# A graph-attention layer's lead-in: constant products, query weights in pieces, four tiles' queries first, and an earlier adjacency pass

## The chip, the cores and the metric

The kernel runs on one core of a Trainium2 chip. A core has five engines that run side by side, each through its own list of instructions in order: TensorE (PE, matrix products, with its weight loads PEld), VectorE (DVE), ScalarE (ACT), GpSimd (POOL) and SyncE (SP, which here only issues transfers). Transfers (DMA) are issued by SP, ScalarE and GpSimd. The engines wait for each other and for transfers by semaphores. The metric is the device time of one execution in microseconds (us); less is better.

## What is computed

One graph-attention layer over 16 batches of 1024 nodes with 512 features, with a residual and a layer normalisation without gain:

```python
# x (16, 1024, 512) f32, adj (1024, 1024) of 0 and 1, Wq Wk Wv Wo (512, 512), biases (512)
q = (x @ Wq + bq).reshape(b, n, 8, 64)
k = (x @ Wk + bk).reshape(b, n, 8, 64)
v = (x @ Wv + bv).reshape(b, n, 8, 64)
scores = einsum('bqhd,bkhd->bhqk', q, k) / sqrt(64)
scores = scores + (1.0 - adj)[None, None, :, :] * -1e9
attn = softmax(scores, axis=-1)
out = einsum('bhqk,bkhd->bqhd', attn, v).reshape(b, n, 512)
x = layernorm(x + out @ Wo + bo)          # mean and variance over the last axis, eps 1e-5
```

The adjacency is sparse and the same for all batches; a query has few keys, some have none.

## The kernel before

**Sorting the queries.** Because the adjacency is sparse, the kernel computes no full score matrix. It first sorts the 1024 queries by their number of keys. The generator `ranks` (L461) loads the eight adjacency tiles of 128 rows and makes one pass over them: `most` (L456) multiplies a tile with the column numbers and takes the eight largest on VectorE (`keys`, `asked`), and sums the row on ScalarE (`key_of`). From the sums it makes a sort key per query (L474), spreads the keys by TensorE (`pkeys`, L479) and copies them on ScalarE (L481), counts for each query on VectorE how many keys are smaller (L491, one instruction per tile of queries), and scatters the rows of `asked` to `order` in memory by these ranks (L485). Then TensorE turns the ranks (`pranks`, L503), and SP reads `order` back as `ranked` (L504). `asked_row` (L511) then says which query stands where, and gathers of everything else use it.

**Edges.** Queries with many keys get further lists: `edges(t)` (L637) for tiles 7 and 6 gathers the adjacency rows of the sorted tile (`codes`, L641), takes the largest again and again on VectorE, and turns edges into rows of keys and queries with small products on TensorE (`poff`, `pe`, `pof`), one-hot sums on VectorE (L711 to L723) and a copy on ScalarE (L730). `lookups` (L593) gathers the keys' places by GpSimd.

**Queries, keys and values of a batch.** The 1024 rows of x come in eight tiles of 128; `pair(b, j)` (L816) does two tiles. A tile is loaded (L750), turned by four transposes on TensorE and copied on ScalarE to `xT` (`transpose_x`, L752). A product of a tile with a 512 x 512 matrix is four matmuls (`product`, L793). `out_q` (L825) scales a tile of queries and adds the bias on VectorE, and SP writes it to memory. The first pair of the first batch computes keys and values plainly (`plain`, L923; `pk`, `pv`, with the outputs copied on ScalarE). All other pairs use a scheme with fewer products: sums and differences of the tiles and of the weights (`combine`, L780; `T1` to `T4`, L383 to L388) and seven units of two matmuls (`unit`, L948) in the accumulators x, p6, p7, z and p4. Their outputs depend on each other: `e` is copied from x on ScalarE (L969) before x is used again, `w` and `g` are sums on VectorE (L972, L975), and z is used a second time only after the V of the odd tile has been taken from it on VectorE (`out_v1`, L984). Transposes of the next pair stand inside the pair's list.

**Blocks.** The attention itself runs in blocks of 128 (query, key) pairs: GpSimd gathers keys and values, VectorE multiplies and reduces to scores (L1313, L1317), ScalarE takes exponentials and weighs values (L1328, L1341), VectorE or TensorE adds up, and TensorE does the output product (`po`).

**What sets the order.** The kernel writes the order of each engine's instructions itself. A loop over places `n` runs from -39 (`LEAD_IN`) to beyond the last block (L1538); block n belongs to place n, and places below 0 are the lead-in. At each place come, in this order: the functions that earlier ones have planned for this place (`later`, L448; then `later_last`), then units of TensorE's work from the list `fronts` until the place's credit is used up (3.3 us at the assumed costs up to place -14, then 2.0), and then one step of each preparing generator: `loads` (L357), `ranks`, and further on `edges`, `checks`, `lookups` and the bias set-up. A `yield` in a generator ends its step. The constants at the top say at which places these start: `ADJ_AT` has the places of the adjacency pass, `REST_FROM` those of the edges of tiles 7 and 6. A unit may have a condition; if it isn't met, the place ends there. Since each engine works in order, an instruction that has to wait holds up all that stand behind it on its engine.

**Loads.** At place -39 `loads` issues Wq in one transfer of 1 MB and the query bias, on ScalarE's queue; at -38 Wk and Wv in halves (`B11`, `B21`, `B12`, `B22`); five places on, `wo` and ten small transfers that fill rows with zeros (L371 to L380); then come T1, T2 and T3, T4 on VectorE, and the other biases. x's first three tiles are issued by SP at the start, and each further one when a transpose has freed a buffer.

**Buffers.** Accumulators of TensorE for products, transposes and small work (`fill_psum`, L262) are four and go round; a fifth user waits until the first one has been read.

Of the kernel before, what the change touches and what calls it, by code (L numbers as in the profile page):

```python
# [10 lines left out]
F32 = mybir.dt.float32  # L11
# [39 lines left out]
ROWS = 3  # L51
# [4 lines left out]
FRONT_BY = -14  # L56
SEGMENT = 64
TOP = 8
ADJ_AT = {-36: (0,), -35: (1, 2), -34: (3, 4), -33: (5,), -32: (6, 7)}
CHECKS_AT = -27  # L60
BIAS_AT = -8
MORE_RANKS_AT = 1
NORMS_AT = 18
LOOK_FROM = -17
REST_FROM = {7: -24, 6: -6}

PRODUCT = 0.86
SUM = 0.87
# [6 lines left out]
P = 128  # L75
# [103 lines left out]
def kernel(  # L179
# [36 lines left out]
    nc = tc.nc  # L216
    B, N, D = x.shape
    HD = D // HEADS
    NPAIR = D // P
# [22 lines left out]
    W = {}  # L242
# [9 lines left out]
    def load_w(t, w):  # L252
        nc.scalar.dma_start(t, w.rearrange("(c p) e -> p c e", p=P))

    with ExitStack() as main:
# [6 lines left out]
        def fill_psum(name):  # L262
            return psum.tile([P, HALF], F32, tag="fill", name=name, bufs=4)
# [92 lines left out]

        def loads():  # L357

            load_w(W["q"], wq)
            broadcast(bq_bc, bq)  # L360
            nc.vector.tensor_scalar(bq_bc, bq_bc, scale, None, op0=OP.mult)
            yield

            B12[0] = work.tile([P, 2, D], F32, tag="kv", name="b12", bufs=5)
            load_w(B11, wk[0:HD2, :])
            load_w(B21, wk[HD2:D, :])
            load_w(B12[0], wv[0:HD2, :])
            load_w(B22, wv[HD2:D, :])
            for _ in range(5):
                yield  # L370
            load_w(W["o"], wo)  # L371
            for rows in solo_rows + pair_rows:
                for r in range(N, rows.shape[0], N + 1):
                    nc.scalar.dma_start(rows[r:r + 1, 0:D], zeros[0:1, 0:D])
            for i in range(1, ROWS):
                nc.scalar.dma_start(q_rows[i][ds(ONE_KEY * P, P), :], zeros[:, 0:D])
                if i % B >= PAIRED_FROM and not merged(i):
                    nc.scalar.dma_start(q_rows[i][0:P, :], zeros[:, 0:D])
            left = P - 8 * (B - PAIRED_FROM)
            nc.scalar.dma_start(more_rows[P - left:, :], zeros[0:left, 0:D])  # L380
            nc.vector.tensor_scalar(before, place[:, 0:P], -1.0, query[:, 0:1], op0=OP.add, op1=OP.is_gt)
            yield
            nc.vector.tensor_tensor(T1, B12[0], B11, op=OP.subtract)  # L383
            nc.vector.tensor_tensor(T2, B22, T1, op=OP.subtract)
            combined.append(True)
            yield
            nc.vector.tensor_tensor(T3, B22, B12[0], op=OP.subtract)
            nc.vector.tensor_tensor(T4, B21, T2, op=OP.subtract)  # L388
            yield
            broadcast(bo_bc, bo)  # L390
            nc.scalar.dma_start(bias_rows[0:NPAIR, :], bq.rearrange("(c p) -> c p", p=P))
            nc.scalar.dma_start(bias_rows[NPAIR:, :], bk.rearrange("(c p) -> c p", p=P))
            nc.scalar.dma_start(bv_rows, bv.rearrange("(c p) -> c p", p=P))
# [54 lines left out]
        def later(k, fn):  # L448
            plan.setdefault(now[0] + k, []).append(fn)
# [11 lines left out]
        def ranks():  # L461
# [11 lines left out]

            nc.vector.scalar_tensor_tensor(key, asked[:, :, 1], float(N), query, op0=OP.mult, op1=OP.add)  # L474
            nc.vector.tensor_copy(keys.rearrange("p (t q) -> p t q", t=NT), key[:, :, None].to_broadcast([P, NT, P]))
            yield
            pk = [fill_psum(f"pkeys_{i}") for i in range(2)]
            for t in range(NT):
# [273 lines left out]
        def transpose_x(b, t):  # L752
            def pe():
                xs = X.pop((b, t))
                p = fill_psum(f"pxT_{b}_{t}")
                for c in range(NPAIR):
                    nc.tensor.transpose(p[:, ts(c, P)], xs[:, ts(c, P)], ident)  # L757

                def out():
                    XT[b, t] = work.tile([P, D], F32, tag="xT", name=f"xT_{b}_{t}", bufs=4)  # L760
                    nc.scalar.copy(XT[b, t], p)
                    n = b * NT + t + 3
                    if t == 0 and b >= PAIRED_FROM:
                        if not merged(b):
                            BOTH[b // 2] = work.tile([P, 2, NPAIR, P], F32, tag="place", name=f"both_{b}", bufs=1)
                        nc.scalar.copy(
                            BOTH[b // 2].rearrange("p w c (h n) -> p h c w n", h=2)[:, b % 2],
                            p.rearrange("p (c w n) -> p c w n", c=NPAIR, w=2),
                        )
                        sq = work.tile([P, D], F32, tag="ysq", name=f"sq_x_{b}", bufs=1)  # L770
                        nc.scalar.activation(sq[0:LONE, :], xs[0:LONE, :], AF.Square, accum_out=x_norm[0:LONE, b:b + 1])
                    if b * NT + t in STORED:
                        nc.sync.dma_start(residual[b * NT + t], xs)
                        later(2, lambda: load_x(n // NT, n % NT))
                    else:
                        load_x(n // NT, n % NT)
                    if t % 2 and (b, t) != (0, 1):
                        later(1, combine)

                def combine():  # L780
                    s = [work.tile([P, HD2], F32, tag=f"s{i}", name=f"s{i}_{b}_{t}", bufs=1 + i // 4) for i in (1, 2, 3, 4)]
                    x0, x1 = XT[b, t - 1], XT[b, t]
                    nc.vector.tensor_tensor(s[0], x1[:, 0:HD2], x1[:, HD2:D], op=OP.add)
                    nc.vector.tensor_tensor(s[2], x0[:, 0:HD2], x1[:, 0:HD2], op=OP.subtract)
                    nc.vector.tensor_tensor(s[1], s[0], x0[:, 0:HD2], op=OP.subtract)
                    nc.vector.tensor_tensor(s[3], x0[:, HD2:D], s[1], op=OP.subtract)
                    SX[b, t // 2] = s

                later(1, out)

            return [(TRANSPOSE, pe, lambda: (b, t) in X)]

        def product(name, lhs, w, out):  # L793

            def unit(c):
                if c == 0:
                    PS[name] = fill_psum(name)
                p = PS[name]
                nc.tensor.matmul(p, lhs(c), w[:, c, :], start=(c == 0), stop=(c == NPAIR - 1))  # L799
                if c == NPAIR - 1:  # L800
                    del PS[name]
                    later(1, lambda: out(p))

            return [(PRODUCT, lambda c=c: unit(c), None) for c in range(NPAIR)]
# [11 lines left out]
        def pair(b, j):  # L816
# [5 lines left out]
                KV[b, tt[i]] = work.tile([P, 2 * D], F32, tag="kv", name=f"kv_{b}_{tt[i]}", bufs=5)  # L822
                return KV[b, tt[i]]

            def out_q(i, p):  # L825

                assert gathered[0] >= start[max(0, b - ROWS + 1)]
                tag, bufs = ("q", 2) if b or j else ("y", Y_BUFS)
                q = work.tile([P, D], F32, tag=tag, name=f"q_{b}_{tt[i]}", bufs=bufs)
                nc.vector.scalar_tensor_tensor(q, p, scale, bq_bc, op0=OP.mult, op1=OP.add)  # L830
                later(1, lambda: nc.sync.dma_start(q_rows[b % ROWS][ds(tt[i] * P, P), :], q))

            def out_k(i, p):
                kv = new_kv(i)
# [72 lines left out]
            def lhs(i):  # L907
# [3 lines left out]
                product(f"pq_{b}_{tt[i]}", lhs(i), W["q"], lambda p, i=i: out_q(i, p)) if b == 0 or tt[i] != ONE_KEY else []  # L911
                for i in range(2)
            )
            if j == 0 and b >= PAIRED_FROM:
                q0 = []
                if merged(b):
                    q0 = product(f"pq_{b}_0", lambda c: BOTH[b // 2][:, 1, c, :], W["q"], lambda p: out_q(0, p))
                    q0 += lone_product()
# [3 lines left out]
            if (b, j) == (0, 0):  # L922
                def plain(i, name, top, bottom, out):  # L923
                    def unit(c):
                        if c == 0:
                            PS[name] = fill_psum(name)
                        w = top() if c < 2 else bottom
                        nc.tensor.matmul(PS[name], XT[b, tt[i]][:, ts(c, P)], w[:, c % 2, :], start=(c == 0), stop=(c == 3))
                        if c == 3:
                            p = PS.pop(name)  # L930
                            later(1, lambda: out(i, p))

                    return [(PRODUCT, lambda c=c: unit(c), None) for c in range(NPAIR)]

                units = q0 + q1 + xt
                for i in range(2):
                    units += plain(i, f"pk_{i}", lambda: B11, B21, out_k)
                for i in range(2):
                    units += plain(i, f"pv_{i}", lambda: B12[0], B22, out_v)
                return units  # L940
# [53 lines left out]
            units = []  # L994
# [520 lines left out]
        prep.setdefault(LOOK_FROM, []).append(lookups())  # L1515
        with tc.manual_schedule():

            fronts += transpose_x(0, 0) + transpose_x(0, 1)
            fronts_by = []
            for b in range(B):  # L1520
                for j in range(NT // 2):
# [136 lines left out]
```

## Time and profile before

| what | value |
|---|---|
| median of 3 runs | 1845.04 us (1844.67 to 1846.6) |
| profiled execution: its time, its span | 1842.18 us, 1840.4 us |
| TensorE busy | 1798.2 us, 98% of the span |
| VectorE busy | 1693.7 us, 92% |
| ScalarE busy | 1563.2 us, 85% |
| GpSimd busy | 1215.3 us, 66% |
| granted TensorE clock, mean | 0.996 |
| moved by DMA | 558.54 MB, mean 303 GB/s |

A row of the profile that speaks of instructions names the line in the kernel, the engine and the operation, then the tile written and the tiles read, their shapes, and the number of instructions; in brackets stands how long the engine stood idle before it, and what ended that. A row of the waits names who waited for whom, the total, the number of times and the longest. A row of the chain is a start, a length and what ran then: the chain is followed back from the last instruction, at each step to what released it. A matmul of 128x512 in f32 shows as two records. `pp` stands for p6, p7 and p4 alike, and `b`, `t`, `s` for the weights and sums of the scheme.

### The profile page before, as it was taken

Reading aid. Unit: us, or ns where it says so; the run is one execution under the profiler, and the core shown is the slowest. Engines: PE = TensorE matmul, PEld = TensorE weight load, DVE = VectorE, ACT = ScalarE, POOL = GpSimd, SP = SyncE. Lnnn points to the kernel's source line nnn. Section 1 sums busy time; section 2 is a strip of 40 time slices with the busy share of each in tenths; the row PEclk is TensorE's granted clock in tenths of the full one; section 3 lists DMA queues with packets and bytes.
Section 4 is the critical chain, followed back from the end, with each engine's and each line's share of the span. In section 5 each row is a group of like instructions: output and inputs, shape, how many; then the busy total and the mean of one; then the engine's idle time right before and its main releaser. Section 6 shows DMA issues by size and latency. Waiting matters only on the chain.

```text
span 1840.4 us, 25352 instructions
## 1 busy us (share of the span) xinstructions
PE 1798.2 (98%) x5140; PEld 876.2 (48%) x5140; DVE 1693.7 (92%) x3473; ACT 1563.2 (85%) x6183; POOL 1215.3 (66%) x1142
## 2 busy tenths in 40 slices
PE   7999999999999999999999999999999999999997
PEld 3444454554444454444444445444544444444443
DVE  6889889999989999999999999999999999997986
ACT  3637869989889898999889988989799999987886
POOL 1367766766565776767757666677666767665786
PEclk9999999999999999999999999999999999999998
DMA  7358787989889899999988998999989999889995
GB/s 287 106 190 253 256 325 237 346 301 327 308 280 314 295 336 319 344 316 308 347 316 310 346 335 276 343 321 322 339 315 325 314 355 326 306 324 325 338 319 191
DMA packets 198791, 558.54 MB, mean 303 GB/s; under 512 B 33450, under 2 KB 33470, under 8 KB 198626
## 3 DMA queue, kind: packets, MB, share of 16 engines
q0 software_dynamic: 112640, 370.50, 59.3%
q1 hardware_dynamic: 82910, 180.52, 26.2%
q10 hardware_dynamic: 3076, 5.82, 0.9%
q14 instruction: 122, 1.00, 0.2%
q8 instruction: 43, 0.70, 0.2%
HBM read 420.30 MB, written 157.45 MB: 314 GB/s over the span
## 4 chain that ended last, share of the span: by engine, by line
PE 69%; DVE 10%; ACT 9%; DMA 4%; issue 3%; POOL 1%; SPq 0%; POOLq 0%; DVEq 0%; ACTq 0%
PE po L799 17%; PE pq L799 15%; PE pp L956 12%; PE z L956 9%; PE x L956 9%; ACT pv L1341 5%; DVE qk L1313 2%; PE poT L1401 2%; PE pxT L757 2%; PE sum L1367 2%; DVE s L1317 2%; PE sum L1366 2%; DVE pv L1357 1%; ACT sq_k L809 1%; DMA kvg<-kv_pair,place_row 1%
## 5 line engine op out<-in xcount | busy, mean ns | idle before, releaser
L1341 ACT ACTIVATE pv<-kvg,pv 128x64 f32<-128x64 f32 x3600 | 907.5, 341 | 0.0
L1292 POOL DMA_INDIRECT kvg<-kv_pair,place_row x462 | 526.7, 1140 | 307.4 <-ACT pv L1341 99.6
L799 PE MATMUL pq<-wq,xT 128*128 128x512 f32 x792 | 367.8, 596 | 0.0
L1317 DVE TENSOR_REDUCE s<-qk 128x8 f32<-128x512 f32 x530 | 360.7, 681 | 6.8
L799 PE MATMUL po<-wo,oT 128*128 128x512 f32 x792 | 359.3, 594 | 0.7 <-ACT oT L1405 0.7
L1313 DVE TENSOR_TENSOR qk<-qt,kvg 128x512 f32<-128x512 f32 x434 | 297.2, 685 | 1.1 <-DMA kvg<-kv_rows,key_row 0.6
L956 PE MATMUL x<-b,xT 128*128 128x512 f32 x504 | 237.3, 593 | 0.5 <-ACT e L969 0.4
L956 PE MATMUL pp<-t,s 128*128 128x512 f32 x504 | 237.0, 593 | 0.0
L1357 DVE TENSOR_TENSOR pv<-pv,pv 128x520 f32<-128x520 f32 x329 | 228.3, 694 | 4.3 <-ACT pv L1341 4.2
L799 PEld LDWEIGHTS po<-wo,oT 128*128 128x128 f32 x792 | 149.1, 191 | 170.0 <-issue 160.2
L799 PEld LDWEIGHTS pq<-wq,xT 128*128 128x128 f32 x792 | 148.4, 192 | 161.9 <-issue 149.9
L1010 POOL DMA_INDIRECT x<-in_x_dram,asked_row x120 | 133.0, 1108 | 77.8 <-issue 21.3
L1148 POOL DMA_INDIRECT out_dram<-y,asked_row x129 | 146.9, 1139 | 39.1 <-issue 21.2
L1328 ACT ACTIVATE pv<-s,absent 128x8 f32<-128x8 f32 x434 | 127.0, 294 | 44.0 <-DVE s L1317 40.8
L809 ACT ACTIVATE sq_k<-kv 128x128 bf16<-128x128 f32 x512 | 150.8, 301 | 6.4 <-DVE kv L979 3.4
L956 PEld LDWEIGHTS pp<-t,s 128*128 128x128 f32 x504 | 94.7, 191 | 108.1 <-issue 99.4
L956 PEld LDWEIGHTS x<-b,xT 128*128 128x128 f32 x504 | 94.2, 191 | 107.4 <-issue 99.0
L956 PE MATMUL z<-b,s 128*128 128x512 f32 x252 | 119.2, 596 | 7.0 <-DVE kv L984 7.0
L1246 POOL DMA_INDIRECT qg<-q_rows,query_row x96 | 104.4, 1088 | 28.4 <-issue 26.9
L956 PE MATMUL z<-t,s 128*128 128x512 f32 x252 | 118.6, 593 | 0.0
L956 PE MATMUL pp<-t,xT 128*128 128x512 f32 x252 | 118.5, 593 | 0.0
L1134 ACT ACTIVATE y<-y,stats 128x512 f32<-128x512 f32 (+1 forms) x128 | 102.7, 806 | 17.0 <-DVE stats L1129 17.0
(279 smaller groups left out, 2713.0 us busy)
## 6 DMA issues: line engine op xcount, KB each, us to landing
kv_pair<-kv SPq DMA_DIRECT2D x98, 512.0 KB
q_rows<-q SPq DMA_DIRECT2D x106, 256.0 KB
qt<-q_rows SPq DMA_DIRECT2D x98, 256.0 KB
residual<-x SPq DMA_DIRECT2D x83, 256.0 KB
y<-residual SPq DMA_DIRECT2D x83, 256.0 KB
kv_rows<-kv SPq DMA_DIRECT2D x15, 512.0 KB
kvg<-kv_pair,place_row POOLq DMA_INDIRECT x462, 6.9
kv_pair<-kv SPq DMA_DIRECT2D x28, 256.0 KB
```

Source lines behind the costliest of these rows:

```text
L799: nc.tensor.matmul(p, lhs(c), w[:, c, :], start=(c == 0), stop=(c == NPAIR - 1))
L809: nc.scalar.activation(sq, s[:, ts(h, P)], AF.Square, scale=scale, accum_out=sums[:, h:h + 1])
L956: nc.tensor.matmul(R[bank], l[:, ts(c, P)], right[:, c, :], start=(first and c == 0), stop=(c == 1), skip_group_check=True,)
L1010: nc.gpsimd.indirect_dma_start(out=y, out_offset=None, in_=x_rows, in_offset=bass.IndirectOffsetOnAxis(ap=asked_row[:, t:t + 1], axis=0), ...
L1148: nc.gpsimd.indirect_dma_start(out=out_rows[b, t], out_offset=bass.IndirectOffsetOnAxis(ap=rows, axis=0), in_=y, in_offset=None, element_o ...
L1246: nc.gpsimd.indirect_dma_start(out=q, out_offset=None, in_=q_rows[b % ROWS], in_offset=bass.IndirectOffsetOnAxis(ap=rows, axis=0))
L1292: nc.gpsimd.indirect_dma_start(out=KG[n], out_offset=None, in_=rows, in_offset=bass.IndirectOffsetOnAxis(ap=(place_row if b else key_row)[ ...
L1313: nc.vector.tensor_tensor(QK[n], q, KG[n][:, 0:D], op=OP.mult)
L1317: nc.vector.tensor_reduce(S[n], QK.pop(n).rearrange("p (h d) -> p h d", d=HD), axis=AX.X, op=OP.add)
L1328: nc.scalar.activation(PV[n][:, D:], S.pop(n), AF.Exp, bias=bias)
L1341: nc.scalar.activation(pv[:, ts(h, HD)], v[:, ds(D + h * HD, HD)], AF.Copy, scale=pv[:, D + h:D + h + 1])
L1357: nc.vector.tensor_tensor(PV[b, t], PV[b, t], pv, op=OP.add)
```

## The change

Six edits, all of them before place 0:

- Two new units at the head of TensorE's list: `busy(3)`, three 128x512 products of a constant (`neg_one`, spread to 128x128 and 128x512) into an accumulator that nobody reads, then the transposes of tile 0, then `busy(1)`, one such product. The transposes of tile 1 move from there to behind the queries of tile 0.
- Wq is loaded in four transfers of 128 rows each, in place of one.
- The queries of tiles 2 and 3 (`pq_0_2`, `pq_0_3`) move from the second pair's list, where they stood between the units of the scheme, into the first pair's, ahead of its keys. The list is now: queries 0, transposes 1 and 2, queries 1, transposes 3, queries 2, queries 3, keys, values. `when(t, ...)` makes a group wait for the turned tile. `out_q` takes the tile's number from its new parameter.
- `ADJ_AT`: tile 0 of the adjacency pass at place -38 and the last two at -33; before, -36 and -32.
- Two more `yield` between the sort keys (L475) and `pkeys`. With the pass ending one place sooner, the sort keys come one place sooner (-32) and `pkeys` and all that follow in `ranks` one place later (-29 for -30, and so on). `REST_FROM` starts the edges of tile 7 one place later (-23), after `asked_row` is known.
- `loads` waits four places in place of five before `wo` and the zero rows; T1 to T4 and the biases come a place sooner with it.

```diff
+WARM = 3, 1
-ADJ_AT = {-36: (0,), -35: (1, 2), -34: (3, 4), -33: (5,), -32: (6, 7)}
+ADJ_AT = {-38: (0,), -37: (1,), -36: (2,), -35: (3,), -34: (4, 5), -33: (6, 7)}
...
-REST_FROM = {7: -24, 6: -6}
+REST_FROM = {7: -23, 6: -6}
...
-            load_w(W["q"], wq)
+            for c in range(NPAIR):
+                nc.scalar.dma_start(W["q"][:, c, :], wq[ds(c * P, P), :])
...
-            for _ in range(5):
+            for _ in range(4):
                 yield
             load_w(W["o"], wo)
...
             nc.vector.tensor_copy(keys.rearrange("p (t q) -> p t q", t=NT), key[:, :, None].to_broadcast([P, NT, P]))
+            yield
+            yield
             yield
             pk = [fill_psum(f"pkeys_{i}") for i in range(2)]
...
-            def out_q(i, p):
+            def out_q(i, p, j=j):
...
+            if (b, j) == (0, 1):
+                q0 = q1 = []
...
-                units = q0 + q1 + xt
+                def when(t, units):
+                    cost, fn, _ = units[0]
+                    return [(cost, fn, lambda: (0, t) in XT)] + units[1:]
+
+                q2, q3 = (
+                    product(f"pq_0_{t}", lambda c, t=t: XT[0, t][:, ts(c, P)], W["q"], lambda p, t=t: out_q(t % 2, p, 1))
+                    for t in (2, 3)
+                )
+                units = when(0, q0) + transpose_x(0, 1) + xt[:1] + when(1, q1) + xt[1:] + when(2, q2) + when(3, q3)
...
-            fronts += transpose_x(0, 0) + transpose_x(0, 1)
+            def busy(n):
+                def pe():
+                    p = fill_psum(f"busy_{n}")
+                    for _ in range(n):
+                        nc.tensor.matmul(p, neg_one.to_broadcast([P, P]), neg_one.to_broadcast([P, D]), start=True, stop=True)
+
+                return [(0.01, pe, None)]
+
+            fronts += busy(WARM[0]) + transpose_x(0, 0) + busy(WARM[1])
```

More of the change, by code (lines that the diff above doesn't have):

```diff
@@ L823, in new_kv @@
                 return KV[b, tt[i]]
-            def out_q(i, p):
+            def out_q(i, p, j=j):
                 assert gathered[0] >= start[max(0, b - ROWS + 1)]
                 tag, bufs = ("q", 2) if b or j else ("y", Y_BUFS)
-                q = work.tile([P, D], F32, tag=tag, name=f"q_{b}_{tt[i]}", bufs=bufs)
+                t = 2 * j + i
+                q = work.tile([P, D], F32, tag=tag, name=f"q_{b}_{t}", bufs=bufs)
                 nc.vector.scalar_tensor_tensor(q, p, scale, bq_bc, op0=OP.mult, op1=OP.add)
-                later(1, lambda: nc.sync.dma_start(q_rows[b % ROWS][ds(tt[i] * P, P), :], q))
+                later(1, lambda: nc.sync.dma_start(q_rows[b % ROWS][ds(t * P, P), :], q))
             def out_k(i, p):
```

## The prediction

> **What bounds the kernel now.** I read the page first, then who waits for whom on TensorE, then stretches of time, then the chain, then the timelines of the first 150 us. TensorE is busy for 1798.2 of 1840.4 us, so the end moves only by what the lead-in does to TensorE's idle and slow time. The list of TensorE's waits (us in total, times, longest us):
>
> ```profile
> PE pxT L757 <- DMA x<-in_x_dram: 7.1, 2, 4.2
> PE z L956 <- DVE kv L984: 7.0, 5, 3.0
> ...
> PE pk L928 <- DMA b<-in_L_gnn_Wk_dram: 2.0, 1, 2.0
> ...
> PE pranks L503 <- DVE rank_row L495: 1.3, 1, 1.3
> ```
>
> Two waits for x (7.1) and one for the key weights (2.0) are what the change aims at; the second line is what may come in their place. Stretches (TensorE, its weight loads, VectorE, ScalarE, GpSimd busy us; then granted clock, DMA share, GB/s):
>
> ```profile
> 10.00:20.00 10.00, 10.00 (x27) 4.78 (x26) 3.04 (x6) 2.58 (x5) 0.56 (x1) 1.00 1.04 415
> 20.00:30.00 10.00, 8.03 (x15) 3.17 (x14) 9.79 (x11) 4.82 (x10) 0.00 (x0) 0.83 0.82 322
> 30.00:40.00 10.00, 10.00 (x25) 4.47 (x24) 9.83 (x10) 3.73 (x17) 0.00 (x0) 1.00 0.57 188
> 40.00:62.00 22.00, 20.35 (x67) 9.94 (x66) 20.77 (x41) 12.82 (x31) 6.42 (x6) 1.00 0.25 86
> 62.00:120.00 58.00, 58.00 (x157) 26.64 (x157) 47.87 (x149) 28.96 (x88) 23.53 (x24) 1.00 0.42 146
> ```
>
> From 20 to 62 VectorE is as full as TensorE (40.4 of 42 us). From 10 to 20 the transfers are full. After 62 TensorE stands still for nothing until 130. Now the chain:
>
> ```profile
> 60.47 1.26 DVE keys L491 x2
> 61.73 0.08 DVE rank_row L495
> 61.81 0.07 issue
> 61.88 0.27 PE pranks L503
> ...
> 125.86 4.28 DMA codes<-in_adj_dram,asked_row
> 130.21 1.11 issue
> 131.31 0.70 DVE qk L1313
> ...
> 144.18 0.69 DVE kv L984
> 144.92 1.98 PE z L956 x4
> ```
>
> So two stretches belong to VectorE: the sorting of queries (keys, pkeys, ranks; 45 to 62) and the one from the transfer of codes to a V tile (126 to 145). A lead of TensorE at 36 us is worth what these two let through. ScalarE's timeline holds one more limit:
>
> ```profile
> 33.58 3.23 ACTq L376 DMA_DIRECT2D q_rows<-zeros  x2
> 36.85 0.44 ACTq L378 DMA_DIRECT2D q_rows<-zeros  x1
> 37.33 0.46 ACTq L380 DMA_DIRECT2D more_rows<-zeros  x1
> 37.84 1.06 ACT L459 ACTIVATE key_of<-adj 128x1024 f32<-128x1024 f32 x1 [6.27 <-DMA q_rows<-zeros]
> ```
>
> ScalarE issues wo and ten small transfers in a row; the second of the two q_rows issues starts at 36.45, when wo has just landed (36.43 in the trace's record of landings). Everything behind it, the key sums of the adjacency pass included, waits.
>
> **The Trainium skill.** The Trainium skill, "TensorE: Matmul & The Clock Gate", section What's actually happening: half clock after an idle window of about 3.4 us, full after a busy one, windows running freely. The trace agrees: a clock of 0.83 over 20 to 30 is one window of 3.4 us at half, and products run at half pace from 23.3 to 26.7 after the wait for Wk. The Trainium skill, "DMA: Bandwidth & Descriptors", section Issuing engines are not separate DMA queues: all transfers share the same 16 engines and interleave, so earlier requests only reorder bytes. It agrees: share 1.04 at 415 GB/s.
>
> **The change, part by part.**
>
> *Constant products.* Three products, each two passes (a product of 128x512 shows as two records). Cold, passes stand 0.86 us apart (four products = 6.9 us), warm 0.43. They start once neg_one is set (1.0 us) and take 3 x 1.72 = 5.2 cold, some 4.7 if the clock comes up meanwhile. x's first tile landed at 4.05, so its transposes go from 4.18 to 5.7: later by 1.5. But the first query product had waited for the second x tile (8.17) and now follows the first, at 5.7 + 0.5 (transpose) + 0.8 (fourth constant product, which covers the copy) = 7.0 instead of 9.1, and warm. The half pace from 9.1 to 13.1 cost 2.0.
>
> *Wq in four pieces.* The whole landed at 7.48; the pieces use the same queue in order, so the last is there at about 7.5, needed at 9.6: nothing gained or lost but three issues of 0.46 on ScalarE, hidden by its wait for the first transpose.
>
> *Order.* q0 7.0 to 10.5; T1; T2 (x landed at 10.97) to 11.5. The copy of T1 stands behind the first adjacency sum on ScalarE (adjacency tile 0 lands at 10.8, sum 1.15), so q1 starts at about 12.7. q1, T3, q2, q3 end at 23.4, two keys and two values (four products of 3.44) at 37.2. Wk and Wv are asked for 3.4 us sooner (after the first copy, not the second), landing at some 19 and 27, so the waits for Wk (2.0 idle, 1.7 half pace) go. Before, the same work, with q2 and q3 (6.9), was done at 36.5 + 6.9 = 43.4. **TensorE leads by about 6 us here.**
>
> *Adjacency pass.* On VectorE it starts at 10.9 (adjacency 0) instead of 18.7. Work up to the keys: 8 x 2.52 + four query outputs 2.4 + sums of x 1.45 + mask 0.3 + T1 to T4 4.9 + key 0.9 = 30.1, so 41.0 (before: 18.7 to 45.6, without query outputs).
>
> *wo one step sooner.* The run of eleven issues begins at 19 instead of 31, behind Wk and Wv. Bytes up to wo's end: adjacency 4.1 MB, x 1.8, Wq and bq 1.3, Wk and Wv 2.0, wo 1.0, queries 0.6 = 10.8; 1.8 are through at 8.2, the rest at about 400 GB/s: wo lands at 30 to 31. ScalarE is then free at about 32 (1.4 more as before), owes four sums (4.8), two key copies (1.0), two sets of squares (2.4) and two value copies (1.0) before e of the first fast pair: about 42.2. TensorE is there at 40.6 (37.2 + two units of 1.72). Wait 1.6; pkeys, now two places later, start at 42.2 + 1.7 = **43.9 instead of 45.69**.
>
> *Ranks.* From pkeys to the first rank 2.66 (trace). Ranks come by three (3.92). By the order of issue, the V of the odd tile (L984) stands now behind six ranks, g and the sums of x, where it stood behind three: 2.66 + 3.94 + 0.77 + 3.92 + 1.53 + 0.65 = 13.5 after pkeys: 57.4. TensorE, without q1 between the two z units, is there 7.9 after pkeys (1.84 + 1.72 + 0.88 + 1.72 + 1.72) and stands for **5.5 us**, which also costs about 1.2 of half pace (0.3 to 1.7, by where the window lies). Then z and x (3.44): the next unit, pp of the third pair, starts at 43.9 + 13.5 + 3.4 + 1.2 = 62.0. Before: 61.98. The lead is gone: 0.
>
> *Edges of tile 7 one step later.* All its instructions move. Its one-hot block (L711 to L723, 124.7 to 127.4, 2.65 us) ran while VectorE would have waited for the codes of tile 6 anyway (2.70 idle, to 130.17). One step later it stands behind that wait, in the chain to the V at 144.2: **+2.65**. If the codes came late enough to hide it, 0; if TensorE's longer stop there costs half pace too, +4.
>
> Sum: 0 + 2.65 = about +2.7 on the profiled execution: 1842.2 to 1844.9. The median of the runs stands 2.86 above the profiled one, so **1847.7**. Not measurable is within 0.2%, 3.7 us.
>
> **Rivals.**
> 1. *Forecast, no measurable change* (0.42; 1844.5 to 1848.7): as summed.
> 2. *Slower* (0.38; 1849 to 1855): ScalarE's run of issues decides. If wo lands after about 31, the wait for e grows past 2 us, which made the clock fall at 20.5 to 22.7. Then the unit behind e takes 3.4 instead of 1.7, pkeys some 0.8 more, and e itself is about 0.8 later: 2.7 + 3.3 = +6.0, 1851. For it: ScalarE's idle 6.27 for the same reason before; against: stops of 2.5 to 3.2 later in the trace left the clock up.
> 3. *Faster* (0.20; 1837 to 1841.3): ScalarE is not held for wo, e is early, pkeys start at 42.4 (TensorE) and the clock holds: 1.5 + 1.2 gained; the codes' block is hidden or its chain starts as much sooner: about -3 to -6, 1840. For it: keys are ready at 41.0; against: the 5.5 stop doesn't depend on where pkeys start.
> 4. *The change misses its aim* (inside 2): constants hold up x longer than they warm, at most 1.5.
>
> The range 1840.5 to 1853 leaves 0.1 on each side.
>
> **What would show it.** Right: first query product near 7; no wait for Wk; a wait of z for L984 of some 5 us near 57; a 2 us wait for e near 41; pp of the third pair at 61 to 63; the wait for L984 at 145 grown. Wrong: that L984 wait below 2 us, or TensorE still ahead by 4 us at 62, would make it faster; a clock below 1.00 at 40 to 46 as well as at 58 to 62 makes it slower.

## The result and the profile after

The changed kernel is slower, by 0.4%. Its median is 1854.22 us (1852.18 to 1856.41, 6 runs) against 1846.28 us (1844.67 to 1849.85, 6 runs) of the kernel before, measured beside it: ratio 1.0039, 95% interval 1.0029 to 1.0050. The profiled execution took 1856.41 us (span 1854.7), the longest of its six; the one of before, 1842.18, is below all six of its kernel's here. So their difference, 14.2 us, says too much (the medians are 7.9 apart), and I use the two traces for where time goes in the first 150 us.

TensorE is busy for 1808.3 us in a span of 1854.7 (before: 1798.2 of 1840.4). The head of its list of waits:

```profile
PE z L971 <- DVE kv L999: 11.1, 5, 5.3
PE pb L412 <- DVE q L835: 4.2, 1, 4.2
PE x L971 <- ACT e L984: 3.6, 1, 3.6
```

The waits for x and for Wk, which the change aims at, have gone from it. In their place stand a wait of 3.6 us for `e`, one of 5.3 us for the V of the odd tile (line 999, before 984), and one of 4.2 us for a query output. The stretches, columns as before:

```profile
10.00:20.00 10.00, 8.94 (x30) 4.36 (x29) 7.44 (x9) 6.02 (x11) 0.55 (x1) 1.00 1.02 405
20.00:30.00 10.00, 10.00 (x25) 4.46 (x24) 9.83 (x14) 0.00 (x0) 0.00 (x0) 1.00 1.04 410
30.00:40.00 10.00, 9.39 (x22) 3.91 (x21) 9.86 (x10) 5.57 (x11) 0.00 (x0) 1.00 0.46 168
40.00:62.00 22.00, 13.07 (x45) 6.65 (x43) 13.90 (x30) 12.33 (x38) 5.82 (x5) 0.85 0.20 73
62.00:120.00 58.00, 57.41 (x147) 26.02 (x148) 44.26 (x135) 27.97 (x80) 19.38 (x19) 0.97 0.35 119
```

From 20 to 30 ScalarE does nothing at all (0.00). From 40 to 62 TensorE and VectorE both have gaps: 13.07 and 13.90 of 22 us, where before they had 20.35 and 20.77. The clock is 0.85 there. ScalarE's timeline tells why:

```profile
20.97 0.38 ACTq L254 DMA_DIRECT2D wo<-in_L_gnn_Wo_dram  x1
25.86 3.59 ACTq L376 DMA_DIRECT2D kv_rows<-zeros  x2
29.50 1.17 ACTq L376 DMA_DIRECT2D kv_pair<-zeros  x4
32.35 0.86 ACTq L378 DMA_DIRECT2D q_rows<-zeros  x2
...
34.34 1.06 ACT L461 ACTIVATE key_of<-adj 128x1024 f32<-128x1024 f32 x1 [15.23 <-DMA q_rows<-zeros]
```

ScalarE stands for 15.23 us (before: 6.27) with these issues. In the trace's record of landings, the halves of Wk landed at 16.92 and 20.95, those of Wv at 25.79 and 29.20, wo at 32.33. The issue of wo starts 0.02 us after a half of Wk, the first zero row 0.07 after a half of Wv, the `q_rows` issue 0.02 after wo. So ScalarE waits for one landing after the other. The instructions in the trace say why: the issues of SP and ScalarE use eight completion semaphores in turn, and each issue waits until the last transfer with its own semaphore has landed. What follows on TensorE, first before, then after:

```profile
45.69 2.01 PE L479 MATMUL pkeys<-ident,keys 128*128 128x128 f32 x16
...
61.98 1.88 PE L956 MATMUL pp<-t,s 128*128 128x512 f32 x4
```

```profile
45.12 3.67 PE L971 MATMUL x<-b,xT 128*128 128x512 f32 x4 [3.59 <-ACT e L984]
48.63 1.95 PE L483 MATMUL pkeys<-ident,keys 128*128 128x128 f32 x16
...
61.95 3.78 PE L971 MATMUL z<-b,s 128*128 128x512 f32 x4 [5.34 <-DVE kv L999]
67.29 1.88 PE L971 MATMUL pp<-t,s 128*128 128x512 f32 x4
```

The last row is pp of the third pair: 67.29, before 61.98, thus 5.3 us late. Both units behind a stop take 3.67 and 3.78 us in place of 1.88: they run at half clock (in the record of the clock from 45.14 to 48.55 and from 58.79 to 65.62). At 110 the lag is still 5.4. Then, on VectorE at the codes of tile 6, again before and after:

```profile
130.17 1.23 DVE L646 TENSOR_TENSOR codes<-codes,place 128x1024 f32<-128x1024 f32 x1 [2.70 <-DMA codes<-in_adj_dram,asked_row]
```

```profile
136.82 1.23 DVE L650 TENSOR_TENSOR codes<-codes,place 128x1024 f32<-128x1024 f32 x1 [4.88 <-DMA codes<-in_adj_dram,asked_row]
...
139.42 0.68 DVE L835 SCALAR_TENSOR_TENSOR q<-pq,bq_bc 128x512 f32<-128x512 f32 x1
140.02 0.15 DVE L715 TENSOR_TENSOR ee<-placed,pe 128x5 f32<-128x5 f32 x1
```

The codes come 6.65 us later than before (130.17), and the one-hot block (140.02 to 142.66) is now behind them. At the z unit that stood at 144.92 TensorE's lag is 9.3 us. The chain of waits says the same of both places. At the first it goes from the copies of pkeys through the ranks and V to z, at the second from the codes through the query output to pb:

```profile
50.62 0.59 ACT key_of L485
51.21 0.03 issue
51.23 1.30 DVE keys L495 x2
...
61.29 0.61 DVE kv L999
61.90 0.04 issue
61.95 2.08 PE z L971 x2
```

```profile
132.53 4.27 DMA codes<-in_adj_dram,asked_row
136.79 0.03 issue
136.82 0.04 DVE codes L650
...
139.50 0.61 DVE q L835
140.11 0.04 issue
140.16 5.40 PE pb L412 x8
```

The lag stays at 9.2 to 9.4 us up to 550. Most of what this execution adds later comes with windows of half clock, at 560 and 1554; some 1.8 us near 1730 come with waits for a transfer (`oTs`). By the prediction's own way of counting, 1842.18 + 9.3 + 2.86 gives 1854.3 us, the median; that it fits to 0.1 us is luck, since the medians are only 7.9 us apart.

### The profile page after: what moved, and what is told of

The parts are those of the page before. It is cut to its first block, busy times and chain, and to the rows that moved or that the text cites. A ratio compares the mean times of both kernels' runs of the same rounds, so it can differ in the third digit from the quotient of the medians.

```text
span 1854.7 us, 25362 instructions
## 1 busy us (share of the span) xinstructions
PE 1808.3 (97%) x5135; PEld 878.0 (47%) x5148; DVE 1693.1 (91%) x3473; ACT 1563.4 (84%) x6183; POOL 1225.8 (66%) x1142
## 4 chain that ended last, share of the span: by engine, by line
PE 82%; DVE 7%; DMA 4%; ACT 3%; issue 2%; POOL 1%; SPq 0%; ACTq 0%; POOLq 0%; DVEq 0%
PE po L803 20%; PE pq L803 17%; PE pp L971 14%; PE z L971 10%; PE x L971 10%; PE pxT L761 3%; PE poT L1416 2%; PE sum L1382 2%; PE sum L1381 2%; ACT pv L1356 2%; DVE qk L1328 1%; DVE s L1332 1%; DMA b<-in_L_gnn_Wk_dram 1%; DMA oTs<-spill 1%; DMA x<-in_x_dram,asked_row 1%
## 5 line engine op out<-in xcount | busy, mean ns | idle before, releaser
L1307 POOL DMA_INDIRECT kvg<-kv_pair,place_row x462 | 534.5, 1157 | 307.0 <-ACT pv L1356 96.7
L971 PE MATMUL x<-b,xT 128*128 128x512 f32 x504 | 241.9, 603 | 3.7 <-ACT e L984 3.6
```

What stands on the lines that cost most here:

```text
L971: nc.tensor.matmul(R[bank], l[:, ts(c, P)], right[:, c, :], start=(first and c == 0), stop=(c == 1), skip_group_check=True,)
L1307: nc.gpsimd.indirect_dma_start(out=KG[n], out_offset=None, in_=rows, in_offset=bass.IndirectOffsetOnAxis(ap=(place_row if b else key_row)[ ...
```

## The experiments

**My theory** is the prediction's second rival with a better size: ScalarE, held by its run of issues, is late with `e`; TensorE stops and loses its clock; pkeys, the ranks and the V behind them are late by as much; and the edges of tile 7, one step later, add 2.65 us or more. **The rivals**: the loss comes from the order of the queries alone; from the edges alone; or from the blocks after 118 us, whatever the lead-in does. The runs fall into two groups. In the second, every kernel, the one before too, takes some 26 us longer (the kernel before 1872 to 1874 us in place of 1846 to 1847) and stops again and again between 120 and 260 us; there I read only the lead-in and the ratios to the kernel before of the same group. What sets the groups apart is not known. By the numbers on record the first ran on chips 1 and 11 and the second on 2 and 11, so the chip alone doesn't explain it.

**Both kernels once more**, both in the first group.

> The kernel before, unchanged, on the chip of these runs, for a profile to lay the others against. Expected on every theory: the ratio to itself 1.000; pp of the third pair at 62, half clock at 23 to 27 only, codes of tile 6 taken at 130. If the long stops that three and late_zeros showed between 120 and 146 belong to the chip and not to the edits, they are here too: TensorE then stands for some 10 us in that stretch also here, and the later start of three means nothing.

> The changed kernel, unchanged, beside the kernel before on one chip. Expected: ratio 1.003 to 1.005 as in the first comparison; x waits about 3.6 us for e near 45, z waits 5.3 us for V near 62, pp of the third pair at 67 to 69. If the loss were a matter of that one chip, the ratio would be within 0.2% of 1.

The copy of before came to a ratio of 0.9998 (0.9988 to 1.0008). Its profile has pkeys at 45.38, pp of the third pair at 61.71, codes of tile 6 at 130.32 and one window of half clock in the middle, at 1067; the one at 23 to 27 that I expected isn't there. The copy of after: 1857.41 us against 1847.45, ratio 1.0050 (1.0034 to 1.0067). In its profile TensorE waits 2.28 us for `kv` up to 41.2 and 2.49 for `e` up to 46.77, with half clock from 41.93 to 52.17, then 5.34 for V; pp of the third pair starts at 70.39. The loss is real, and the stop around `e` varies from one execution to the next.

**TensorE's part alone.**

```diff
 # from the changed kernel back to the kernel before
-ADJ_AT = {-38: (0,), -37: (1,), -36: (2,), -35: (3,), -34: (4, 5), -33: (6, 7)}
+ADJ_AT = {-36: (0,), -35: (1, 2), -34: (3, 4), -33: (5,), -32: (6, 7)}
-REST_FROM = {7: -23, 6: -6}
+REST_FROM = {7: -24, 6: -6}
-            for _ in range(4):
+            for _ in range(5):
                 yield
             load_w(W["o"], wo)
...
-            yield
-            yield
             yield
             pk = [fill_psum(f"pkeys_{i}") for i in range(2)]
```

> Of the change only TensorE's part: the constant products, Wq in four pieces and the queries of four tiles ahead of the first keys; adjacency pass, wo, pkeys and edges stand where they stood before. Theory A (the order of queries alone pushes the odd V behind six ranks, and wo is asked for later, so that ScalarE is held later): keys ready at 42 to 43, a wait of x for e of 2 us or more, a z stop for V, pp of the third pair at 64 to 65, codes of tile 6 and its block as before; time +2 to +3 us, ratio 1.001 to 1.002. Rival B (the loss is made by the moved transfers and passes, not by the order of the queries): no z stop of over 2 us, pp of the third pair at 60 or sooner, ratio 1.000 or below.

1852.78 us against 1847.45, ratio 1.0026 (1.0016 to 1.0035), thus about half of what the whole change loses in this group. TensorE's timeline, then two rows of ScalarE's:

```profile
42.76 2.02 PE L481 MATMUL pkeys<-ident,keys 128*128 128x128 f32 x16 [3.56 <-DVE keys L477]
...
60.03 3.78 PE L969 MATMUL z<-b,s 128*128 128x512 f32 x4 [5.59 <-DVE kv L997]
...
66.12 1.88 PE L969 MATMUL pp<-t,s 128*128 128x512 f32 x4
```

```profile
34.97 1.06 ACT L461 ACTIVATE key_of<-adj 128x1024 f32<-128x1024 f32 x1 [12.88 <-DMA q_rows<-zeros]
...
45.77 0.60 ACT L982 COPY e<-x 128x512 f32<-128x512 f32 x1
```

There is no wait of TensorE for `e`; it waits for the keys instead, and pkeys still start 2.6 us before those of the copy of before. Yet z stops for 5.59 us, and pp of the third pair is 4.4 us late. With tile 3's queries out of the second pair, TensorE comes to the second z early, and on VectorE V now stands behind all eight ranks (six in the changed kernel, three before). The lag stays 4.3 to 4.4 from 62 to 143 (pb, the bias product, at 134.90 against 130.50), so without the edges' edit nothing is added there. ScalarE's rows show something that I had not looked for. With wo in its old place ScalarE is held as well, until 34.97 (34.34 in the changed kernel), and `e` is even later. But here pkeys stand ahead of the x unit that waits for `e`, and so don't feel it. So wo's earlier place is not what makes the hold. By the order of TensorE's list, what lets the hold reach pkeys is their own later place (the two added `yield`), behind that unit; no run takes this edit alone. Of my expectations the wait for `e` failed and the stop for V came out; pp of the third pair (64 to 65 expected) and the ratio (1.001 to 1.002) both came out worse.

**Tile 3's queries back in the second pair**, all else as changed.

```diff
-                q0 = q1 = []
+                q0 = []
...
-                    for t in (2, 3)
+                    for t in (2,)
-                units = when(0, q0) + transpose_x(0, 1) + xt[:1] + when(1, q1) + xt[1:] + when(2, q2) + when(3, q3)
+                units = when(0, q0) + transpose_x(0, 1) + xt[:1] + when(1, q1) + xt[1:] + when(2, q2)
```

> The changed kernel with the queries of tile 3 back in the second pair, between the two uses of z; those of tile 2 stay in front. Theory A (V of the odd tile stood behind six ranks because z came one place later, with nothing between the two uses of z): z comes a place sooner, V ahead of all ranks, and the stop of z for L984 (now 5.3 us) is under 1 us; but TensorE is at e 3.4 us sooner and waits for it about 7 us, and the ranks now stop it at pranks by about 2; the time falls by only 1.5 to 4. Rival (the stop belongs to the sorting as such, wherever V stands): a stop of 4 us or more stays between 50 and 62, and the time is within 1.5 us of 1854.

In the second group: ratio 1.0043 (1.0031 to 1.0055). The stop for V has gone, but the wait for `e` is longer, since TensorE comes sooner:

```profile
45.30 3.78 PE L971 MATMUL x<-b,xT 128*128 128x512 f32 x4 [5.90 <-ACT e L984]
...
54.33 1.95 PE L483 MATMUL pkeys<-ident,keys 128*128 128x128 f32 x16
...
70.12 0.27 PE L507 MATMUL pranks<-ident,rank 128*8 128x128 f32 x1 [1.78 <-DVE rank_row L499]
```

pp of the third pair is at 64.75, 4.4 us sooner than in edges_sooner (further down), which has the changed kernel's lead-in and is in the same group (69.13). But in TensorE's list, now shorter, pkeys come to stand behind one more pp, the transposes and a z, and the ranks are turned only 2.4 us sooner (70.12; 72.56 in edges_sooner). The ratio is no better than that of edges_sooner (1.0039): alone, this edit shows no gain in time.

**The zero rows later**: the ten issues behind wo go ten places on, so that ScalarE is not held. (Shown for `kv_rows` and `kv_pair`; those of `q_rows` and `more_rows` move with them.)

```diff
             load_w(W["o"], wo)
-            for rows in solo_rows + pair_rows:
-                for r in range(N, rows.shape[0], N + 1):
-                    nc.scalar.dma_start(rows[r:r + 1, 0:D], zeros[0:1, 0:D])
...
             nc.scalar.dma_start(bv_rows, bv.rearrange("(c p) -> c p", p=P))
+            for _ in range(7):
+                yield
+            for rows in solo_rows + pair_rows:
+                for r in range(N, rows.shape[0], N + 1):
+                    nc.scalar.dma_start(rows[r:r + 1, 0:D], zeros[0:1, 0:D])
...
```

> The changed kernel with the ten small issues of zero rows moved from place -34 to -24; wo stays. Theory A (ScalarE, held in its run of issues until wo has landed, makes e late, and with e the sort keys' products): ScalarE is free at 21, e is there before TensorE asks (40.6), the wait of x for e (3.6) and of pp for the key copy (0.6) go, the half-clock window at 45 goes too; pkeys start at 42 to 43 in place of 48.6, pp of the third pair at 60 to 61.5 in place of 67.3; the time falls by 5 to 7 us, to 1847 to 1849. Rival (VectorE's sorting sets the end of this stretch whatever e does): pkeys move, but the third pair starts within 1 us of 67.3, and the time stays within 1.5 us of 1854.

Ratio 1.0020 (1.0007 to 1.0033) in the second group. The changed kernel itself wasn't run there, so whether the expected 5 to 7 us are gained stays open; the ratio is below that of edges_sooner (1.0039), but the intervals overlap. The lead-in is compared:

```profile
42.08 1.95 PE L485 MATMUL pkeys<-ident,keys 128*128 128x128 f32 x16
...
55.40 3.78 PE L973 MATMUL z<-b,s 128*128 128x512 f32 x4 [5.34 <-DVE kv L1001]
61.05 1.88 PE L973 MATMUL pp<-t,s 128*128 128x512 f32 x4
```

No wait for `e`; pkeys come 6.8 us before those of edges_sooner in the same group (48.84), pp of the third pair 8.1 us (69.13). So the late `e` and its half clock come from the issues on ScalarE: that is shown. The stop for V is the same 5.34 us to the hundredth: it doesn't depend on when pkeys start.

**The edges of tile 7.** First one step sooner in the changed kernel, then one step later in the kernel before, in each of the groups.

```diff
 # edges_sooner, in the changed kernel
-            for _ in range(3):
+            for _ in range(3 - (t == 7)):
 # edges_only and edges_again, in the kernel before
-REST_FROM = {7: -24, 6: -6}
+REST_FROM = {7: -23, 6: -6}
```

> The changed kernel with one of the three empty places after the gather of tile 7's codes taken out, so that all later steps of its edges stand where they stood before the change. Theory A (the one-hot block of tile 7 stands behind the wait for tile 6's codes): VectorE does the block while it waits for these codes, TensorE's stop ahead of the bias product at 140 falls from 4.2 by 2 to 2.7, and the half-clock window at 140 may go with it (up to 1.7 more); the time falls by 2.5 to 4. Rival (the codes' own lateness decides, and the block only fills a gap somewhere else): within 1 us of 1854.

> The kernel before with one edit of the change: edges of tile 7 one step later (REST_FROM 7 at -23). Theory A (the prediction's step): up to 125 us identical; the one-hot block of tile 7 (2.65 us of VectorE) runs behind the wait for tile 6's codes, V of the pair that ends near 145 comes 2.65 us later; time +2.6 us, ratio 1.0014. Rival B (the codes of tile 6 arrive later or VectorE has slack there): 0, ratio 1.000. By the kernel with TensorE's part alone, whose lag stays at 4.4 us from 62 to 143, nothing but this edit and the lead-in adds lag there.

> The kernel before with edges of tile 7 one step later, once more, since on the chip of its first run the stretch from 120 to 260 is disturbed in every kernel. Theory A: lag 0 up to 125, the codes of tile 6 taken as late as before or up to 1.3 us later, its one-hot block of 2.65 us behind them, lag +2.65 from 145 to the end; ratio 1.0014. Rival B: 0, ratio 1.000.

edges_sooner, in the second group: ratio 1.0039 (1.0022 to 1.0056), with the changed kernel's lead-in (wait for `e` 3.59, for V 5.34); nothing can be read from its stretch behind 120, so it settles nothing. edges_only: 1.0019 (1.0005 to 1.0033) there; edges_again, in the first: 1848.56 us against 1846.81, ratio 1.0011 (0.9999 to 1.0022). That is 2.0 us, with 2.65 inside and 0 just inside; the ratio of edges_only excludes 0. VectorE and TensorE in edges_again, with TensorE's row in the copy of before last:

```profile
131.47 1.22 DVE L646 TENSOR_TENSOR codes<-codes,place 128x1024 f32<-128x1024 f32 x1 [3.71 <-DMA codes<-in_adj_dram,asked_row]
...
134.07 0.68 DVE L830 SCALAR_TENSOR_TENSOR q<-pq,bq_bc 128x512 f32<-128x512 f32 x1
134.67 0.15 DVE L711 TENSOR_TENSOR ee<-placed,pe 128x5 f32<-128x5 f32 x1
```

```profile
134.81 6.19 PE L410 MATMUL pb<-wo,bvb 128*128 128x512 f32 x8 [4.20 <-DVE q L830]
```

```profile
130.50 3.70 PE L410 MATMUL pb<-wo,bvb 128*128 128x512 f32 x8 [0.79 <-ACT sums L730]
```

The next V of an odd tile (L984) is taken at 148.12, in the copy of before at 144.63: 3.5 us late. Of that, 1.15 were there at the codes already, 1.0 even at 118 (none was expected up to 125), and 0.4 at the ranks, which the edit does not touch. But it is late in two ways. On VectorE the one-hot block stands ahead of g, as predicted. On TensorE the bias product pb takes its place ahead of the last of the one-hot products, so its accumulator is no longer one that ScalarE has read (0.79 us of wait) but the one of a query, which is read only behind the codes. The three stops that the copy of before has here (0.79, 1.84 and 1.36) become one of 4.20, with half clock behind it: pb takes 6.19 us instead of 3.70. The two ways end within a microsecond of each other, and the runs don't tell which of them sets the end.

**All three together.**

```diff
+            for _ in range(7):
+                yield
...
-                q0 = q1 = []
+                q0 = []
-            for _ in range(3):
+            for _ in range(3 - (t == 7)):
...
```

(the three edits above, the ten issues ten places later)

> All three of these edits together. Theory A, with the parts adding up along one chain: no wait for e, pkeys at about 43, no stop of z for L984, pranks at about 60 (70.7 in the changed kernel), block of tile 7 in its old place: 11 + 2.7 less than 1854, so 1840 to 1842, and 4 to 6 below the kernel before. Rival (the three stops stand in for each other, so that taking all away leaves VectorE's sorting as the bound): 1846 to 1848, no better than before.

> The changed kernel with three of its parts taken back together (the ten zero rows issued ten places later, tile 3's queries back in the second pair, edges of tile 7 one step sooner). Theory A (the lead-in and the edges explain the loss, as the prediction's steps have it): no wait for e, no stop of z for V, pp of the third pair some 7 us before that of the kernel before, and a time below the changed kernel's by 0.3 to 0.5%, thus within 0.2% of the kernel before or below it by up to 0.3%, as far as the block from 118 to 147 lets the lead through. Theory B (a cause from the block from 118 to 147 on, untouched by these edits): within 0.1% of the changed kernel.

Ratio 0.9996 (0.9977 to 1.0015), and in the first group 1.0000 (0.9989 to 1.0012): 1847.37 against 1847.45 us, 10 us less than the copy of after beside it. So mending these three places takes back the whole loss. The constant products, the four pieces of Wq, the earlier adjacency pass and wo's earlier place are all still in this kernel; on balance they cost nothing. As to the rivals: the order of the queries alone loses 5.3 us (tensor_only) and the edges alone some 2, so neither is the whole; and no loss of the blocks' own is left. But nothing is gained against the kernel before, as the rival of the first expectation had it: in three_again x of the third pair starts at 52.90 in place of 58.44, pranks at 59.99 in place of 61.60, and at 85 VectorE is 1.2 us behind. The late zero rows have a price here; on ScalarE:

```profile
61.03 0.57 ACTq L391 DMA_DIRECT2D kv_pair<-zeros  x2
67.21 0.84 ACTq L393 DMA_DIRECT2D q_rows<-zeros  x2
...
69.92 1.15 ACT L635 ACTIVATE adj<-adj,neg_one 128x1024 f32<-128x1024 f32 x1 [8.89 <-DMA q_rows<-zeros]
```

**The zero rows in a gap of ScalarE.** At 41 to 45 ScalarE only waits for pkeys (4.62 us in three_again). The kernel spread is three with the ten issues two places behind the biases; spread_keys also has pkeys one place sooner; before_zeros moves the issues in the kernel before. Of the diff, the second part is spread_keys alone.

```diff
-            for _ in range(7):
+            for _ in range(2):
                 yield
...
-            yield
             yield
             yield
             pk = [fill_psum(f"pkeys_{i}") for i in range(2)]
```

> The kernel before with one edit: the ten zero-row issues taken from behind wo and put two places behind the bias rows (some 41 us), so that ScalarE is not held for wo at 31 to 38. Theory A (VectorE is full from 20 to 62 and sets the ranks there): ScalarE's hold of 6.27 us goes, pkeys still start at 45 to 45.7, pp of the third pair at 62, time 0 to -1 us, ratio 0.9995 to 1.000. Rival B (ScalarE's hold already cost the kernel before): pkeys at 44 or sooner, the third pair's pp at 60 or sooner, time -1.5 us or more.

> As the three parts taken back together, but with the zero rows two instead of seven places behind the bias rows. There they held ScalarE for 8.9 us from 61 to 70 behind the load of the ranked queries, the copies of x and of keys behind them, VectorE for 3.8 and TensorE for 2.2 us, and the lead of 1.6 us at the ranks was gone by 85 us. Theory A (that hold ate the lead): no stop of ScalarE of over 3 us between 60 and 72, the first codes taken 1.5 us before the kernel before takes them (76.5), 1.5 us ahead at 110; time -1 to -2 us against the kernel before, ratio 0.9989 to 0.9995. Rival B (the way from ranks to codes has its own clock, or 118 to 147 takes the lead): ratio 1.000.

> As the kernel spread, and the keys' transposes (pkeys) one place sooner. VectorE waited 1.7 us for their copies at 45 in the kernel with three parts taken back, with keys ready at 41.4 and pkeys at 44.2. Theory A (the ranks then start 1.7 us sooner, and VectorE sets the end of the lead-in): pkeys at 42.5, pranks at 58.3 against 61.6 in the kernel before; some 3 us ahead at 110, time -2 to -3.3 us, ratio 0.998 to 0.999. Rival B (V of the first fast pair or the copies of x take VectorE's place): no more than spread.

> The kernel spread once more, for the same reason. It was 2.5 us ahead at 108. Theory A (the lead-in alone decides the rest): 1.5 to 2.5 us ahead from 145 to the end, ratio 0.9986 to 0.9992. Rival B (the stretch from 118 to 147 has its own limit, GpSimd's gathers and their landings): ratio 1.000, TensorE standing there as much longer as it came sooner.

> The kernel spread_keys once more, for the same reason. It was 3.05 us ahead at 108. Theory A: 2 to 3 us ahead from 145 to the end, ratio 0.9984 to 0.9990. Rival B: ratio 1.000, the lead lost between 118 and 147.

before_zeros: ratio 1.0003 (0.9987 to 1.0019); pkeys at 45.53 behind a wait of 0.79 for the keys, pp of the third pair at 61.86. In the kernel before, ScalarE's 6 us are free: VectorE sets the keys. (This kernel also shows the second group: with nothing changed behind 62, its VectorE is 1.0 us behind that of the copy of before at 108 and 25.2 at 240.)

spread: 0.9985 (0.9970 to 0.9999), and in the first group 1843.28 us against 1846.81, ratio 0.9984 (0.9975 to 0.9992). It beats the kernel before, by 0.16%, and with it the changed one. ScalarE issues the ten in one go and is back for the copies of pkeys at 45.25; the first codes are taken at 73.87, in the copy of before at 76.53. ScalarE in spread_again:

```profile
42.78 0.46 ACTq L395 DMA_DIRECT2D q_rows<-zeros  x1
43.28 0.53 ACTq L397 DMA_DIRECT2D more_rows<-zeros  x1
45.25 0.59 ACT L487 COPY key_of<-pkeys 128x512 f32<-128x512 f32 x1 [4.61 <-PE pkeys L485]
```

Its VectorE leads that of the copy of before by 2.6 us at 108 and by 3.6 at 152: the lead passes the blocks, against rival B. spread_keys: 0.9986 (0.9973 to 1.0000) and 0.9984 (0.9974 to 0.9993). In spread_keys_again pranks come at 57.63 and not at 59.95, but no time is gained: GpSimd now issues a gather of x (66.86) ahead of the first codes (68.18), which are taken only at 74.67, behind a wait of 2.86 us for their landing. What TensorE and VectorE gain there goes into the order of GpSimd's queue.

## Why the prediction was wrong

- **Constant products, order, loads: right.** The first query product starts at 6.58 (7.0 forecast), queries of tile 1 at 12.07 (12.7), the values end at 37.06 (37.2), the keys are ready at 41.94 (41.0). No wait for x or Wk is left. The first of these is luck in part: in tensor_only the clock came up later and the first query product started at 7.96.
- **The step that failed is the time at which ScalarE is free and `e` is there, in the part "wo one step sooner".** The path was right: the run of issues, then ScalarE's work, then `e`, then pkeys. The sizes were too small. wo landed at 32.33, where I had 30 to 31: by then 11.3 MB had been moved and not 10.8, at a mean of 384 GB/s from 8.2 on and not 400. Four issues stood behind it, not three as before, and took 2.0 us, not 1.4, so ScalarE was free at 34.34, where I had 32: +2.3. The bias rows, which the change brings a place sooner, held it for another 1.20 up to 42.36; I gave them nothing. Against these 3.5 stands a slip: the forecast's own terms add up to 41.8 with the copy of `e`, not to 42.2. `e` was done at 45.07: +2.9. The wait came to 3.6 in place of 1.6. The half clock behind it, which the forecast put at nothing and only the second rival named, made the x unit take 3.5 us up to pkeys for 1.7: +1.8. pkeys: 43.9 + 2.9 + 1.8 = 48.6, measured 48.63. The name of that part misleads, though: tensor_only has the hold without the earlier wo.
- **Ranks and the V behind them: right.** From pkeys to the end of V 13.3 us (13.5 forecast), the stop 5.34 (5.5). The half clock behind it cost 1.9, not 1.2. So pp of the third pair came at 67.29, not 62.0: the sum "lead gone: 0" became +5.3. Without the hold (late_zeros) the rest of the forecast comes out: the stop for V is 5.34 and pp is at 61.05.
- **Edges: the block was right, the sum too small.** 2.65 was forecast. TensorE's lag grew by 3.9, from 5.4 at 110 to 9.3 at the z unit of 145. The forecast's alternative, +4 if a longer stop of TensorE there costs half pace too, is what came: half clock from 140.71 to 144.12. But the stop was not the one that was looked for. The wait of z for V, 1.06 before, did not grow but went; the stop stood ahead of pb, whose accumulator I hadn't followed.
- **The rival "slower" had the mechanism**: it named the landing of wo after 31 and the fall of the clock, and summed +3.3 for the lead-in and +6.0 in all, 1851. The traces have 5.3 and 3.9, the medians are 7.9 apart, and the time came out 3 us above 1851. I had given it 0.38, too little: my landing estimate of "30 to 31" stood directly at its threshold of "after about 31". What I held against it was misread, too: not all stops of 2.5 to 3.2 us left the clock up, for the one of 3.09 that ends at 1808.33 has half clock behind it, from 1808.47 to 1811.89. The prediction's sign for slower, a clock below 1.00 at 40 to 46 and at 58 to 62, came. The case "faster" fell with the hold.
- **"The lead is gone" held in the main**: of TensorE's lead little gets past VectorE's ranks. In three_again, 5.5 us at the third pair's first unit were 1.6 at pranks.

## What to carry to other kernels

When a step of issues is moved earlier, ask for each issue which landing it waits for; where the transfers are full, the last of these landings sets when the issuing engine is free, and an engine that also computes stands still until then. Then ask what stands behind that engine's late work: here it hurt only where the sort keys' products had been put behind it. Small transfers that nobody needs soon belong into a gap of the issuing engine's own work: ten of them cost TensorE a stop of 3.6 us and its clock in one place, gave it back in another, and the place that looked latest and safest held ScalarE for 8.9 us again. And work that is taken out of a later stage, here tile 3's queries, may have been the cover of another engine's chain there: it came back as a stop of 5.3 us.

## What the runs showed of the hardware

- The Trainium skill, "TensorE: Matmul & The Clock Gate", section What's actually happening, has half clock behind an idle window of about 3.4 us, with windows that run freely. In these traces the periods at half are 3.41 us or a multiple, but for the first and the last, which the ends cut. But the stop that costs can be shorter than a window: a gap of 2.77 us between two starts of products, near 545 to 563, is in the traces of before and after and in the seven others of the first group. Behind it the clock stayed up before and fell for 3.41 us after (560.55 to 563.96). Among the others it fell there in tensor_only, edges_again and spread_again, and not in the two copies, three_again and spread_keys_again.
- Three constant products (six records from 1.07) brought the clock up at 4.18 us in the profile of after, at 6.96 in tensor_only and at 7.16 in spread, with the same three products: 3 us of spread that a forecast of this size has to allow for.
